# Eight image pairs through four layers on one core: layer 3 fed from padded copies, with the next pair's first scan step made inside it

## The chip, the cores and the metric

The kernel runs on one core of one Trainium2 chip. The metric is device time in microseconds (us). Five engines work beside each other, each through its own queue of instructions: TensorE (PE, matmul), VectorE (DVE), ScalarE (ACT), GpSimd (POOL) and SyncE (SP), which here only issues DMA transfers. SBUF is the on-chip memory of 128 partitions; PSUM holds what PE accumulates.

## What is computed

The input is 16 images of 192 channels and 64 x 64 points in float32. Four layers follow each other, each added to its own input, each with a group norm (32 groups of 6 channels) ahead of it:

```python
x = x + L0(gn(x))   # a small per-channel network: sigmoid differences
x = x + L1(gn(x))   # five shifted copies, 1x1 convolution 960 -> 192
x = x + L2(gn(x))   # selective scan, K = 4 directions, N = 16 states
x = x + L3(gn(x))   # depthwise convolutions, pointwise, batch norm, clip
```

The change is about the end of L2 and about L3:

```python
# L2: h = exp(delta * A) * h + delta * u * B ;  y = sum over n of C * h
# L3:
y = dw3x3(v) + dw5x5(v) + dw1x7(v) + dw7x1(v)
z = pointwise(y)                       # 192 -> 192
z = (z - mean(z)) / sqrt(var(z) + eps) # over all 16 images
return clip(gamma * z + beta, 0, 6)
```

## The kernel before, in words

**Tiling.** Two images of 192 channels make a pair of 384 rows: three tiles (NT = 3) of 128 partitions by 4096 points. There are eight pairs. After weights are prepared, `front(0)` does layers 0 and 1 and the projections of pair 0. Then `pair()` (L1161) runs for each pair `scans` (L783 to L1052) and `layer3` (L1053 to L1159). At the end the batch-norm sums of all pairs are combined and 24 tiles are streamed once more (L1230).

**Scans.** The loop has 768 steps: 3 tiles j, 4 directions, 4 chunks of 1024 points (48 values of t, the step's tile, direction and chunk) and 16 states n. A step is: `product` on DVE (pbt times du), `scan` on DVE, a copy of the last state on ACT, h times cb on POOL, a DMA that accumulates every fourth h onto its neighbour, and sums on PE into ysum, which ACT copies to X or Xt (Xt holds the transposed directions). Before each t, `step_rest` makes delta (PE matmul of dt, softplus on ACT) and du (POOL, delta times the normalised xn). All of this goes through wrappers (`_InOrder`, L51 and L64) that keep each engine's queue in program order, so that the profile gives one line, L64, to all of it. The front of the next pair is interleaved in the same loop, some instructions per step.

`finish(j)` closes a tile: four adds of Xt (transposed) to X, on POOL for tiles 0 and 1 and on DVE for tile 2, bn_stats of the sums on DVE, and the store of X to x3_d in DRAM. For tiles 0 and 1 it is spread over ten steps of the following tile; for tile 2 it stands behind the loop. The xn of the first tile is loaded and normalised, and the first delta and du are made, ahead of the loop; the first cb, bp and dt are loaded there too.

**Layer 3.** Here the instructions are not kept in program order: a scheduler places them on the queues. The parts are:

- xp (L1064): the three tiles are loaded from x3_d into the middle of 70 x 70 images, rows of 64 floats, whose edges POOL zeroes (L1070, L1072).
- diag (L1075): for each tile PE_TAPS = 7 diagonal matrices of 128 x 128, built on POOL from the identity, 21 instructions.
- `group_norm` (L337 to L369): bn_aggr on DVE, sums over groups on PE twice (gn_sum, 14 small matmuls each), small DVE operations between, and the power that gives rstd on POOL. `normalise` (L319) then works on DVE, in place, tile by tile.
- four chunks c of 1024 points, in each the three tiles j. The 29 taps are divided: 7 on PE as matmuls with the diagonals (L1111, two halves of 512 points), 8 on POOL (GP_TAPS; ACT scales a window, L1102, POOL adds it to g, L1106), and 14 on DVE (L1129), which adds to the PSUM tile l_p and writes the last sum to l_y. Four ident matmuls bring g into l_p (L1123).
- the pointwise matmuls zp (L1143) from the three l_y, a copy by ACT (L1150), bn_stats (L1151, zst) and the store of z to z_d (L1152).

One matmul instruction of float32 is two records in the trace. The PSUM tiles l_p have two buffers, the pointwise ones four banks. Memory is handed from one pool to the next, so that the first writer of a new tile waits for the last reader of what lay there.

Of the kernel before, what the change touches and what calls it, by code (L numbers as in the profile page):

```python
# [48 lines left out]
TAPS = [(3, 0), (3, 6), (0, 3), (6, 3)] + [(y, x) for y in range(1, 6) for x in range(1, 6)]  # L49
PE_TAPS = 7  # L50
GP_TAPS = 8  # L51
# [53 lines left out]
def conv_preact_kernel(ctx: ExitStack, tc: tile.TileContext, a: dict):  # L105
# [13 lines left out]
    wm_d = dram.tile([P, NG, P + GR], F32, name="wm_d")  # L119
    wt_d = dram.tile([GR, NG, 2 * P], F32, name="wt_d")  # L120

    const = ctx.enter_context(tc.tile_pool(name="const", bufs=1))
# [78 lines left out]
    with tc.tile_pool(name="prep", bufs=1) as prep, tc.tile_pool(  # L201
# [83 lines left out]
        for part, w in (  # L285
            (wc[:, :, 2:5, 2:5], w3x3),
            (wc[:, :, 3, :], w1x7),
            (wc[:, :, :, 3], w7x1),
        ):
            nc.vector.tensor_tensor(part, part, w, ALU.add)  # L290


# [16 lines left out]

    sets = [Made(n) for n in range(2)]  # L310

    def image(ap):
# [23 lines left out]

    def group_norm(E, st, stat, ps, gm, rstd):  # L337

        mv = stat.tile([P, NT, 2], F32, name="mv", tag="mv")
        mean = stat.tile([P, NT], F32, name="mean", tag="mean")  # L340
        d2 = stat.tile([P, NT], F32, name="d2", tag="d2")
        half = stat.tile([P, NT], F32, name="half", tag="half")
        E.dve.memset(half, -0.5)
        for j in range(NT):
            E.dve.bn_aggr(mv[:, j, :], st[:, j, :, :].rearrange("p c s -> p (c s)"))
        E.dve.tensor_copy(mean, mv[:, :, 0])

        def mean_of(src):
            s = ps("gn_sum")
            for jo in range(NT):  # L350
                for n, (b, ji) in enumerate(INTO[jo]):
                    E.pe.matmul(
                        s[:, jo : jo + 1],
                        grp[:, b, :],
                        src[:, ji : ji + 1],
                        start=(n == 0),
                        stop=(n == len(INTO[jo]) - 1),
                    )
                yield
            return s[:, :NT]  # L360

# [419 lines left out]

    def scans(i, o, st3, nxt):

        E = _Engines(tc, True)
        with ExitStack() as es:

            def pool(name, bufs, **kw):
                return es.enter_context(tc.tile_pool(name=name, bufs=bufs, **kw))

            one = pool("l2one", 1)  # L790
            two = pool("l2two", 2)
            hp = pool("l2h", 8)
# [6 lines left out]

            X = one.tile([P, L], F32, name="X")  # L800
            Xt = one.tile([P, L], F32, name="Xt")
# [16 lines left out]

            def load_bp(t):
                if t < T:  # L820
                    j, k, at, first = todo[t]
                    bps[t] = two.tile([BP, LC], BF16, name="bp")
                    E.sp.dma_start(out=bps[t], in_=o.bp[k, :, at : at + LC])

            def load_dt(t):
                if t < T:
                    j, k, at, first = todo[t]
                    dts[t] = one.tile([32 + RD, 512], F32, name="dt")
                    src, r = (o.dtp, RD * (k // 2)) if k % 2 else (o.dt, RD * (2 + k // 2))
                    for h in range(2):  # L830
                        E.sp.dma_start(
                            out=dts[t][32 * h : 32 * h + RD, :],
                            in_=src[r : r + RD, at + 512 * h : at + 512 * h + 512],
                        )

            def load_xn(j):
                if j < NT:
                    xns[j] = one.tile([P, L], F32, name="xn")
                    E.sp.dma_start(out=xns[j], in_=row_tiles(o.x2)[:, j, :])
# [27 lines left out]
            def step_rest(t):  # L867


                j, k, at, first = todo[t]  # L870
                dt = dts.pop(t)
                v = py.tile([P, LC], F32, name="v", tag="ysum")
                for h in range(2):
                    rows = slice(32 * h, 32 * h + RD)
                    E.pe.matmul(
                        v[:, 512 * h : 512 * h + 512],
                        dtw[rows, k, j, :],
                        dt[rows, :],
                        start=True,
                        stop=True,  # L880
                    )
                delta = two.tile([P, LC], F32, name="delta")
                E.table(SOFTPLUS)
                E.act.activation(delta, v, AF.Softplus, bias=dtb[:, k, j : j + 1])
                yield
                du = two.tile([P, LC], F32, name="du")
                E.gps.tensor_tensor(image(du), image(delta), seq(xns[j], k, at, LC), ALU.mult)
                made[t] = delta, du
# [74 lines left out]
            def finish(j):  # L963
# [12 lines left out]
                for at in range(10):  # L976
                    if at in (0, 2, 4, 6):
                        add(at // 2)
                    if at in (3, 5, 7, 9):
                        E.later(lambda c=at // 2 - 1: stats(c))  # L980
                    yield
                E.sp.dma_start(out=row_tiles(x3_d[i])[:, j, :], in_=X)

            load_xn(0)
            load_dt(0)
            load_bp(0)
            norm_xn(0)
            for _ in step_rest(0):
                pass
            load_dt(1)  # L990
            for s in range(3):
# [6 lines left out]
            fin = iter(())  # L998
            gstep = iter(())
            for s in range(total):  # L1000
                t, n = divmod(s, N)
# [3 lines left out]
                if n == 2:  # L1005
                    load_bp(t + 1)
                if n == 4:
                    load_dt(t + 2)
                if n == 6:
# [12 lines left out]
                if n > 4:  # L1022
                    next(fin, None)


# [22 lines left out]
            for g in (finish(NT - 1), fr):  # L1048
                for _ in g:
                    E.between()  # L1050
            E.between()

    def layer3(i, st3):  # L1053
        E = _Engines(tc, False)
        with tc.tile_pool(name="l3s", bufs=1) as stat, tc.tile_pool(name="l3x", bufs=1) as xk, tc.tile_pool(
            name="l3w", bufs=1
        ) as w_, tc.tile_pool(name="l3", bufs=2) as wk, tc.tile_pool(
            name="l3_pt", bufs=2, space=PSUM
        ) as pt, tc.tile_pool(name="l3_pz", bufs=4, space=PSUM) as pz:
            S = HW + 6  # L1060
            xp = xk.tile([P, NT, S, S], F32, name="xp")
            inside = slice(3, 3 + HW)
            for j in range(NT):
                nc.sync.dma_start(  # L1064
                    out=xp[:, j, inside, inside], in_=image(row_tiles(x3_d[i])[:, j, :])
                )
            pw = load("pw", [P, len(BLOCKS), P], w_)
            diag = w_.tile([P, NT, PE_TAPS, P], F32, name="diag")
            for edge in (slice(0, 3), slice(3 + HW, S)):
                nc.gpsimd.memset(xp[:, :, edge, :], 0.0)  # L1070
                for j in range(NT):
                    nc.gpsimd.memset(xp[:, j, inside, edge], 0.0)  # L1072
            for j in range(NT):
                for t, (ty, tx) in enumerate(TAPS[:PE_TAPS]):
                    nc.gpsimd.tensor_scalar(  # L1075
                        diag[:, j, t, :], ident, wc[:, j, ty, tx : tx + 1], None, ALU.mult
                    )
            gm = stat.tile([P, NT], F32, name="gm")
            rstd = stat.tile([P, NT], F32, name="rstd")
            banks = lambda name: pz.tile([P, 512], F32, name=name, tag="ps")  # L1080
            for _ in group_norm(E, st3, stat, banks, gm, rstd):
                pass
            for j in range(NT):
                v = xp[:, j, inside, inside]
                normalise(nc.vector, v, v, gm, rstd, j)
            zst = stat.tile([P, NT, 8, 6], F32, name="zst")
            def window(j, c, rows, tap):
                return xp[:, j, c + tap[0] : c + tap[0] + rows, tap[1] : tap[1] + HW]

            def factor(j, tap):  # L1090
                return wc[:, j, tap[0], tap[1] : tap[1] + 1]

            own = PE_TAPS + GP_TAPS
            for c in range(4):
                ys = []
                for j in range(NT):
# [59 lines left out]
            for j in range(NT):  # L1156
                nc.vector.bn_aggr(zmv[:, j, :], zst[:, j, :, :].rearrange("p c s -> p (c s)"))
            nc.sync.dma_start(out=zstat_d[i], in_=zmv.rearrange("p j s -> p (j s)"))

    def pair(i, q, more):  # L1160

        with tc.tile_pool(name="st3", bufs=1) as p3:
            st3 = p3.tile([P, NT, 8, 6], F32, name="st3")
            scans(i, sets[q], st3, None if more is None else (more, sets[1 - q]))
            layer3(i, st3)

    with tc.tile_pool(name="f_ps", bufs=1, space=PSUM) as ps:
        for _ in front(0, sets[0], _Engines(tc, False), Banks(ps, 8), True):
            pass
    for i in range(npair):  # L1170
        pair(i, i % 2, i + 1 if i + 1 < npair else None)

# [166 lines left out]
```

## Time and profile before

| | us |
|---|---|
| median of 3 runs | 28018.27 (28016.04 to 28032.98) |
| the profiled execution, its time | 28007.89 |
| its span, first to last instruction | 28006.0 |
| last scan of pair 0, end | 4172.6 |
| first scan of pair 1, start | 4538.5 |
| last scan of the last pair, end | 27270.8 |
| last zst of the last pair, end | 27617.3 |

The profiled execution is one run of the program under the hardware profiler; its rows are in microseconds from the first instruction. A row of the timeline gives start, length, engine, line, operation, what it writes and reads with shapes, how many instructions it joins, and in brackets the idle time ahead of it with what ended it. A row of windows gives a stretch and each engine's busy time in it, the clock that TensorE was granted as a share of the full one, and the share of DMA time. The mean granted clock of the run is 0.912.

In the scans a step takes 3.57 to 4.2 us. DMA is busy for 0.61 to 0.92 of the time there, more where the front of the next pair runs. Layer 3 takes four chunks of some 66 us with an opening ahead and a closing behind.

### The profile page before, as it was taken

What the parts mean: (1) busy time and instruction counts of PE and PEld (TensorE: products, weight loads), DVE (VectorE), ACT (ScalarE), POOL (GpSimd) and SP (SyncE); (2) the same over time, 40 slices, a digit from 0 to 9 for tenths busy, and PEclk for the clock granted to TensorE, in tenths of its full rate; (3) what the DMA queues carried; (4) which work ended last, traced back from release to release, by engine and by line L of the source; (5) the groups of instructions that cost most, each with busy time, mean ns of one, the idle gap of its engine ahead of it and who ended that gap; (6) DMA issues with size and microseconds to landing.
All of it is one profiled execution on the core that took longest, in us unless ns stands there. A gap on an engine that the chain in (4) does not pass through costs nothing. (4 is left out here: it accounts for less than half of the span.)

```text
span 28006.0 us, 208082 instructions
## 1 busy us (share of the span) xinstructions
PE 23305.0 (83%) x57140; PEld 9559.7 (34%) x57140; DVE 24196.3 (86%) x15397; ACT 16122.6 (58%) x23044; POOL 20813.2 (74%) x10440
## 2 busy tenths in 40 slices
PE   8799977999689986999779997899968998676663
PEld 4343323333233332333324332333323333222221
DVE  0399988999899998999989998899989999899994
ACT  7388445774468643785548844577446864344433
POOL 2388877887778876888768887788777887677772
PEclk9899988999899998999889998899989999888886
DMA  4489864898568973898748986589856897367765
GB/s 100 132 222 224 215 201 141 220 220 220 157 181 226 220 220 116 220 224 219 212 124 222 224 215 202 141 221 220 219 155 182 226 219 218 114 189 192 192 183 234
DMA packets 2008001, 5448.00 MB, mean 195 GB/s; under 512 B 550392, under 2 KB 550616, under 8 KB 1989424
## 3 DMA queue, kind: packets, MB, share of 16 engines
q1 hardware_dynamic: 1782192, 4578.95, 56.4%
q0 software_dynamic: 221184, 805.40, 15.2%
q10 hardware_dynamic: 3456, 50.33, 0.4%
q8 instruction: 455, 7.45, 0.1%
q14 instruction: 714, 5.85, 0.1%
HBM read 3896.19 MB, written 329.51 MB: 151 GB/s over the span
## 5 line engine op out<-in xcount | busy, mean ns | idle before, releaser
L64 POOL TENSOR_TENSOR h<-h,cb 128x1024 f32<-128x1024 f32 x6144 | 14856.3, 2464 | 4181.8 <-ACT state L64 3664.7
L64 DVE TENSOR_TENSOR_SCAN h<-dA,state,pbt 128x1024 f32<-128x1024 f32 x4608 | 10809.9, 2346 | 675.9 <-ACT dA L64 91.2
L64 PE MATMUL ysum<-h,ident 128*128 128x512 f32 x18432 | 9464.1, 639 | 208.2 <-DMA h<-h 138.6
L64 DVE TENSOR_TENSOR pbt<-du,pbt 128x1024 f32<-128x1024 f32 x6144 | 7434.8, 1210 | 658.0 <-PE pbt L64 619.6
L64 ACT ACTIVATE dA<-delta,t_alog 128x1024 f32<-128x1024 f32 x6144 | 7036.6, 1146 | 4.9
L64 PEld LDWEIGHTS ysum<-h,ident 128*128 128x128 f32 x18432 | 3777.4, 206 | 4520.3 <-issue 3923.8
L64 ACT COPY state<-h 128x1 f32<-128x1 f32 x6144 | 1145.0, 186 | 6401.7 <-DVE h L64 6324.1
L64 PE MATMUL pbt<-bp,pick 96*128 96x512 bf16 x8192 | 2686.3, 412 | 2127.4 <-DVE h L64 2106.9
L64 DVE TENSOR_TENSOR_SCAN h<-dA,pbt 128x1024 f32<-128x1024 f32 x1536 | 3509.1, 2285 | 228.5 <-DMA h<-h 52.6
L64 PE MATMUL p<-t,wts 96*128 96x512 f32 x5376 | 2707.6, 602 | 136.1 <-ACT t L64 135.9
L64 PE MATMUL p<-m,wms 128*96 128x512 f32 (+1 forms) x5376 | 2653.6, 595 | 0.9 <-ACT lu L64 0.3
L64 ACT ACTIVATE t<-p,bias 96x512 f32<-96x512 f32 x2688 | 1809.2, 679 | 1046.2 <-PE p L64 1027.8
L64 PEld LDWEIGHTS <-pick 96*128 96x128 bf16 x8192 | 711.9, 101 | 4920.9 <-DVE h L64 3256.2
L1106 POOL TENSOR_TENSOR l_g<-l_g,l_m 128x1024 f32<-128x1024 f32 x672 | 1615.1, 2405 | 452.3 <-ACT l_g L1102 346.6
L64 PE MATMUL l_p<-l_xp,w1s 128*128 128x512 f32 x3920 | 1844.7, 599 | 3.4 <-POOL l_xp L64 3.3
L1129 DVE SCALAR_TENSOR_TENSOR l_p<-xp,wc,l_p 128x1024 f32<-128x1024 f32 x1248 | 1589.8, 1287 | 262.6 <-PE l_p L1123 231.7
L64 PE MATMUL pbt<-bp,pick_mix 96*128 96x512 bf16 x4096 | 1282.7, 395 | 559.6 <-DVE h L64 555.3
L64 POOL DMA_DIRECT2D h<-h x1536 | 1359.0, 885 | 494.9 <-POOL h L64 427.9
L1111 PE MATMUL l_p<-xp,diag 128*128 128x512 f32 x2688 | 1289.0, 639 | 332.0 <-DVE l_y L1129 281.3
L64 PEld LDWEIGHTS p<-t,wts 96*128 96x128 f32 x5376 | 1007.9, 190 | 1292.6 <-issue 903.8
L64 ACT ACT_TABLE_LOAD x1111 | 1425.4, 1283 | 19.4
L64 POOL TENSOR_TENSOR du<-delta,xn 128x1024 f32<-128x1024 f32 x384 | 1034.5, 2694 | 452.7 <-ACT delta L64 452.7
(219 smaller groups left out, 17750.1 us busy)
## 6 DMA issues: line engine op xcount, KB each, us to landing
cb<-cp_d SPq DMA_DIRECT2D x2048, 512.0 KB
cb<-c_d SPq DMA_DIRECT2D x2048, 512.0 KB
h<-h POOLq DMA_DIRECT2D x1536, 512.0 KB, 7.1
cb<-cp_d SPq DMA_DIRECT2D x2048, 256.0 KB
cb<-c_d SPq DMA_DIRECT2D x2048, 256.0 KB
m<-l_xn SPq DMA_DIRECT2D x3072, 128.0 KB
bp<-bp_d SPq DMA_DIRECT2D x384, 192.0 KB
f0x<-in_x SPq DMA_DIRECT2D x96, 512.0 KB
```

The lines of the kernel that those rows point to most:

```text
L64: return self._tc.keep_in_program_order(call(*args, **kw))
L1106: nc.gpsimd.tensor_tensor(g, g, m, ALU.add)
L1111: nc.tensor.matmul(ps[:, cs], diag[:, j, t, :], window(j, 16 * c + 8 * h, 8, tap), start=(t == 0), stop=False,)
L1129: nc.vector.scalar_tensor_tensor(image(y if tap is TAPS[-1] else ps), window(j, 16 * c, 16, tap), factor(j, tap), image(ps), ALU.mult, ALU ...
```

## The change

- PE_TAPS is 8 instead of 7: DVE has 13 taps a tile and chunk.
- The diagonals are made once, in the preparation, stored to diag_d (1.57 MB) and loaded in each layer 3.
- xp_d in DRAM holds zero-padded 70 x 70 images of tiles 0 and 1. It is zeroed once. `finish` stores four strips of 16 rows (128 x 16 x 64) of each finished tile into it, beside the store to x3_d. Layer 3 loads tiles 0 and 1 whole from it.
- X lives on into layer 3: tile 2 is normalised from it straight into its padded image, and its store to x3_d is issued there.
- A second group norm over tiles 0 and 1 (gn0) is interleaved with the last 13 steps of the scans. No group of channels that tile 0 holds reaches tile 2, so tile 0 is normalised with it at once, in four strips of 16 rows.
- `begin(o_next)` loads the next pair's first xn, dt and bp and makes its delta and du; it is called ahead of chunk 2 of layer 3, and once behind `front(0)`. X, xn, bp, dt, delta and du lie in a pool `over` that lasts over all pairs.

```diff
-PE_TAPS = 7
+PE_TAPS = 8
...
+        zero = prep.tile([P, S, S], F32, name="zero")
+        nc.vector.memset(zero, 0.0)
+        for j in range(NT - 1):
+            nc.sync.dma_start(out=xp_d[j], in_=zero)
+        for j in range(NT):
+            diag = prep.tile([P, PE_TAPS, P], F32, name="diag", tag="diag", bufs=2)
+            for t, (ty, tx) in enumerate(TAPS[:PE_TAPS]):
+                nc.gpsimd.tensor_scalar(
+                    diag[:, t, :], ident, wc[:, j, ty, tx : tx + 1], None, ALU.mult
+                )
+            nc.sync.dma_start(out=diag_d[:, j, :, :], in_=diag)
...
+    def begin(o, psum):
+        E = _Engines(tc, False)
+        k = ORDER[0]
+        xn = over.tile([P, L], F32, name="xn")
+        nc.sync.dma_start(out=xn, in_=row_tiles(o.x2)[:, 0, :])
+        dt = load_dt(nc.sync, o, k, 0)
+        bp = load_bp(nc.sync, o, k, 0)
+        normalise(nc.vector, xn, xn, o.gm, o.rstd, 0)
+        delta = over.tile([P, LC], F32, name="delta", tag="delta", bufs=2)
+        make_delta(E, psum(), delta, dt, k, 0)
+        du = over.tile([P, LC], F32, name="du", tag="du", bufs=2)
+        nc.gpsimd.tensor_tensor(image(du), image(delta), columns(xn)[:, : LC // HW, :], ALU.mult)
+        return xn, bp, delta, du
...
                     if at in (3, 5, 7, 9):
-                        E.later(lambda c=at // 2 - 1: stats(c))
-                    yield
-                E.sp.dma_start(out=row_tiles(x3_d[i])[:, j, :], in_=X)
+                        c = at // 2 - 1
+                        E.later(lambda c=c: stats(c))
+                        if j < NT - 1:
+                            rows = slice(3 + 16 * c, 19 + 16 * c)
+                            E.sp.dma_start(
+                                out=xp_d[j][:, rows, 3 : 3 + HW],
+                                in_=image(X[:, 1024 * c : 1024 * c + 1024]),
+                            )
+                    yield
+                if j < NT - 1:
+                    E.sp.dma_start(out=row_tiles(x3_d[i])[:, j, :], in_=X)
...
+            gm0, rstd0 = (p3.tile([P, NT], F32, name=f"first{n}") for n in range(2))
+            gn0 = group_norm(E, st3, p3, ps, gm0, rstd0, range(2))
...
+                if t == T - 1 and n > 2:
+                    next(gn0, None)
...
-            xp = xk.tile([P, NT, S, S], F32, name="xp")
             inside = slice(3, 3 + HW)
-            for j in range(NT):
-                nc.sync.dma_start(
-                    out=xp[:, j, inside, inside], in_=image(row_tiles(x3_d[i])[:, j, :])
-                )
+            xps = {j: xk.tile([P, S, S], F32, name=f"xp{j}") for j in (2, 0, 1)}
+            for j in range(NT - 1):
+                nc.sync.dma_start(out=xps[j], in_=xp_d[j])
+            for r in range(0, HW, 16):
+                v = xps[0][:, 3 + r : 19 + r, inside]
+                normalise(nc.vector, v, v, gm0, rstd0, 0)
+            diag = w_.tile([P, NT, PE_TAPS, P], F32, name="diag")
+            nc.sync.dma_start(out=diag, in_=diag_d)
             pw = load("pw", [P, len(BLOCKS), P], w_)
-            diag = w_.tile([P, NT, PE_TAPS, P], F32, name="diag")
+            nc.sync.dma_start(out=row_tiles(x3_d[i])[:, NT - 1, :], in_=X)
...
-            for j in range(NT):
-                v = xp[:, j, inside, inside]
-                normalise(nc.vector, v, v, gm, rstd, j)
+            v = xps[1][:, inside, inside]
+            normalise(nc.vector, v, v, gm, rstd, 1)
+            normalise(nc.vector, xps[2][:, inside, inside], image(X), gm, rstd, 2)
...
+            begun = None
             for c in range(4):
+                if c == 2 and o_next is not None:
+                    begun = begin(o_next, lambda: pt.tile([P, 1024], F32, name="l3_p"))
```

## The prediction

> **What bounds the kernel now.** I read the busy table first, then the windows over the first pair's boundary (last scan of a pair to the first scan of the next), then its timeline, then DVE's waits.
>
> ```profile
> PE 23305.0 (83%) x57140; PEld 9559.7 (34%) x57140; DVE 24196.3 (86%) x15397; ACT 16122.6 (58%) x23044; POOL 20813.2 (74%) x10440
> ```
>
> DVE carries the kernel: its scans and products fill the 768 steps of a pair. The rest of a pair, layer 3, looks different. Columns: the stretch, its length, then busy time of each engine, granted clock, DMA share, GB/s.
>
> ```profile
> 4172.60:4218.80 46.20, 13.75 (x42) 8.76 (x41) 16.62 (x23) 1.20 (x2) 17.01 (x30) 0.61 0.44 120
> 4218.80:4320.60 101.80, 76.53 (x168) 30.60 (x170) 63.64 (x49) 52.45 (x49) 86.22 (x35) 0.86 0.17 42
> 4320.60:4386.90 66.30, 58.10 (x138) 23.24 (x136) 57.34 (x48) 31.20 (x30) 49.52 (x21) 0.92 0.06 24
> 4386.90:4452.60 65.70, 57.50 (x138) 23.06 (x136) 57.34 (x48) 31.07 (x30) 49.54 (x21) 0.92 0.06 24
> 4452.60:4519.30 66.70, 46.81 (x106) 18.45 (x102) 58.44 (x52) 10.09 (x13) 16.49 (x7) 0.85 0.06 26
> 4519.30:4538.50 19.20, 3.98 (x8) 1.04 (x8) 4.00 (x3) 5.90 (x6) 2.85 (x1) 0.53 0.62 218
> ```
>
> These sum to 365.9 us: an opening of 46.2 in which no engine is half busy, four chunks, and a closing of 19.2 in which the next pair's first step is loaded and made. The seven such gaps are 365.9 to 366.8, mean 366.2; the last pair, with no successor, needs 346.5 from its last scan to its last zst. The opening and the chunk that follows it, by their timeline (start, length):
>
> ```profile
> 4171.65 8.74 POOL L1075 TENSOR_SCALAR diag<-ident,wc 128x128 f32<-128x128 f32 x15
> ...
> 4180.37 2.33 POOL L64 TENSOR_TENSOR h<-h,cb 128x1024 f32<-128x1024 f32 x1
> ...
> 4197.15 0.32 SPq L64 DMA_DIRECT2D x_d<-X  x1
> 4203.46 20.00 SPq L1064 DMA_DIRECT2D xp<-x_d  x3
> ...
> 4218.78 14.73 PE L1111 MATMUL l_p<-xp,diag 128*128 128x512 f32 x28 [6.18 <-DVE xp L319]
> ...
> 4243.79 6.59 DVE L1129 SCALAR_TENSOR_TENSOR l_p<-xp,wc,l_p 128x1024 f32<-128x1024 f32 x5 [13.27 <-PE l_p L1123]
> ```
>
> The diagonals stand on POOL ahead of the last h multiply; behind that come the sums (to 4199.45), the store of X, the load of what was stored, its normalisation (4216.31, 2.41), and POOL's eight taps. DVE starts its taps 71.2 after the last scan (4172.6). Times below with a plus count from that scan.
>
> **The opening.** In the built order of the changed kernel POOL runs the last h multiply at once: it ends at +2.6 instead of +10.1. PE's sum (3.54), ACT's copy (1.01) and DVE's adds and statistics (12.07) follow as now, to +19.3. Tile 0 loads from xp_d as soon as the multiply has released its memory; the nearest row, 2 MB of contiguous xn, takes 9.1 from issue to normalisation, so it is there at about +12. Its four strips take 2.5 (2.41 as one), to +21.8. The full group norm takes 8.9 to the end of its second PE sums as now: +30.7. Tile 0's conv stands behind them on PE: 32 records of 128x512 instead of 28 at 0.44, 2.3 of cold clock, 1.93 for the ident matmuls, so DVE's first tap is at +49.3. POOL has g(j0) by +44.4 (two adds before the rstd power, five behind it, 2.4 each), inside that. Tile 1 and 2 are normalised (3.45 and 3.93) in DVE's wait. Gain so far 21.9.
>
> **The first chunk** is now paced by POOL, 86.2 busy of 101.8, since each tile's g costs 19.3 there. POOL starts 25 earlier and ends g(j2) at +83; I get the end of chunk 0 at +114.3 against +149.3, 35.0 earlier.
>
> **The eighth tap.** A steady chunk of before, first DVE's, then PE's part:
>
> ```profile
> 4409.77 13.21 DVE L1129 SCALAR_TENSOR_TENSOR l_p<-xp,wc,l_p 128x1024 f32<-128x1024 f32 x10
> 4423.01 1.28 DVE L1129 SCALAR_TENSOR_TENSOR l_y<-xp,wc,l_p 128x1024 f32<-128x1024 f32 x1
> 4426.59 2.61 DVE L1129 SCALAR_TENSOR_TENSOR l_p<-xp,wc,l_p 128x1024 f32<-128x1024 f32 x2 [2.30 <-PE l_p L1123]
> ```
> ```profile
> 4410.00 14.68 PE L1111 MATMUL l_p<-xp,diag 128*128 128x512 f32 x28 [7.65 <-DVE l_y L1129]
> 4424.61 1.93 PE L1123 MATMUL l_p<-l_g,ident 64*64 64x512 f32 x8
> ```
>
> DVE loses three instructions of 1.29 a chunk, 3.9. But the ring it sits in closes through PE: tile 2's conv waits for a PSUM buffer that l_y of tile 0 frees, and takes 14.68 for 28 records, 2.3 of it a cold start after 7.65 idle (the mean over 24 such gaps; after gaps under 1.5 nothing is lost). With 32 records it adds 1.75. In the new order the next conv is also cut by the pointwise matmuls: 12 of its 16 instructions stand ahead of them, 4 behind, 3.5 on the path from l_y of tile 2 to the next tap. PE's idle gap shrinks to some 4, so I give the cold start 0.8. Ring: 35.4 from the chunk's first tap to tile 2's, 20.35 for that tile, 9.2 to the next: 65.0, against 65.7 to 66.7. Nearly all of the tap is given back; without the cut it would be 61.5.
>
> [...]
>
> **The closing.** xn, dt, bp are fetched in the scans, and delta and du are made between chunks 1 and 2. The first scan of the next pair now waits only for the last z store to land: 7.2 from the last l_y to its issue, 3.4 to its landing, where before 27.1 lay between that l_y and the scan. In exchange chunk 1 to 2 waits: delta stands on ACT behind three scaled windows, one waiting for POOL, and its PSUM buffer is the one that tile 0's conv needs, whose last nine instructions stand behind four pointwise ones. I get 14.4 more for that chunk. So chunk starts are +114.3, +193.7 (65.0 + 14.4), +258.7; tile 2's taps +294.1, l_y +312.3, first scan +323. Against 366.2: **-43.2** a pair, -302 for seven. The last pair has no such step: 114.3 + 130 + 35.4 + 18.25 + 8.25 = 306.2 against 346.5, -40.
>
> **What moves into the scans.** DVE does the xn normalisation (3.3, between the 2.41 and 3.47 of its rows) and the small operations of the early group norm (2.3) where its pitch leaves no room: 3.56 to 3.60 in the last steps for 1.21 + 2.35. That is +5.6 for seven pairs and 2.3 for the last: +41. The loads fall where DMA is at 0.61 and cost nothing; if they did, their 9.1 would come back. Diagonals and zeroing in the opening weights delay POOL by some 6 to 9, which the early start of pair 0's first step (xn load to scan 16.5, about 7.5 saved) pays back: +2, between -8 and +10.
>
> **The strips.** Four stores per tile into xp_d, 128x16x64 of 256-byte rows, eight a pair, on SP's queue ahead of the cb loads, each waiting for its X add on POOL (for whose lateness the next cb load, two steps ahead, has some 7). The trace of before has no store of such rows. Its loads of 256-byte packets (layer 1's windows, 239616 of them) take 24 ns a packet: 2048 / 16 x 25 ns = 3.2 a strip. Ends: nothing if hidden, 25.6 a pair if all is exposed. The stretch of tile 0's strips has little room, that of tile 1's has:
>
> ```profile
> 8870.00:9860.00 990.00, 919.78 (x2344) 387.32 (x2343) 926.70 (x565) 655.15 (x966) 835.53 (x424) 0.97 0.92 220
> 9860.00:10690.00 830.00, 677.00 (x1631) 270.43 (x1630) 758.47 (x469) 399.19 (x572) 630.62 (x309) 0.90 0.73 213
> ```
>
> I take two thirds of tile 0's four: 8.5 a pair, 1 in the last: +60.
>
> [...]
>
> **Sum.** -302 - 40 + 41 + 2 + 60 = -239 on the profiled 28007.9 (span 28006.0): 27769. The median shown is 10.4 above the profiled time, so **27780**.
>
> **Rivals.** (1) Strips hidden and the cold start gone: -60 and some -26 (0.8 a chunk): 27690. (2) PE is worse than I built it: the cold clock costs its full 2.3 in each ring (+1.5 x 32 = 48) and begin 8 more a pair (+56): 27885. DVE's 13.3 wait behind PE speaks for it, the shorter gap against. (3) The other side: strip stores at over 4.7 each. Without them the change is worth 299, 37.4 a pair; eight at 4.7 eat it, at 5.5 the kernel is slower by over 0.2%; at 6.4, twice the load's packets, it is 27719 (the sum without strips, at the median) + 8 x 8 x 6.4 = 28130. The 0.92 of DMA speaks for it, the 0.73 of tile 1's stretch and the 24 ns against. (4) Padded copies that come no earlier, because the load of tile 0 waits for memory held to the end of the sums: tile 0 is then ready at +19.3 + 9.1 + 2.5 = +31, PE no later than forecast but POOL's chain 8 later, 64 in all: 27845.
>
> **How the numbers follow.** The forecast with what lies between it and (4): 0.62; (1) 0.13; (2) or strips at the full 25.6 (+120, 27900): 0.12; between these and no change counted with no change, 0.06; (3) 0.07. Range 27680 to 27910. 0.2% is 56 us, about what a measurement of this kernel can tell from no change: faster 0.87, same 0.06, slower 0.07.
>
> **What would show it.** In the profile after: first l_p at +49 (wrong above +56), chunk cycle 65, the chunk with delta 79, gaps of 323; in the scans the steps behind 272 longer by 8, those behind 528 not. A chunk of 61.5 would refute the cut conv, unchanged steps behind 272 the price of the strips, and a gap above 340 the closing.

## The result, and the profile after

The changed kernel takes 28164.89 us (median of 5, 28149.86 to 28170.34) against 28018.27 for the kernel before: a ratio of 1.0051, 95% interval 1.0036 to 1.0065. It is slower, by 147 us; forecast were 238 us less. The profiled execution has a span of 28148.1, 142.1 more than before.

The share of busy time tells nothing of it:

```profile
PE 23517.4 (84%) x57652; PEld 9661.5 (34%) x57652; DVE 24161.9 (86%) x15398; ACT 16120.1 (57%) x23044; POOL 20709.2 (74%) x10272
```

DVE does less work than before (24161.9 against 24196.3) in a longer span. I cut both traces at the same instructions, the first and last scan of each pair. The gaps between pairs are 352.1 to 353.6 now (365.9 to 366.8 before), so layer 3 did become shorter, by 13.3 a pair and, in the last pair, by 12.8 to its last zst and 14.4 to the end of the program: 108 in all, a third of the 342 forecast. The scans became longer, by 247 in eight pairs. These are the windows over the same boundary as before:

```profile
4210.00:4241.80 31.80, 11.78 (x42) 8.30 (x41) 18.12 (x25) 7.82 (x8) 7.99 (x7) 0.66 0.76 288
4241.80:4341.00 99.20, 79.44 (x177) 32.17 (x178) 62.94 (x48) 45.83 (x43) 82.40 (x34) 0.87 0.03 11
4341.00:4419.60 78.60, 61.75 (x144) 24.52 (x143) 54.05 (x46) 33.33 (x32) 52.37 (x22) 0.87 0.05 20
4419.60:4493.40 73.80, 67.17 (x160) 27.39 (x159) 54.10 (x46) 30.94 (x30) 49.56 (x21) 0.95 0.05 22
4493.40:4558.50 65.10, 52.41 (x125) 20.65 (x124) 54.24 (x48) 10.06 (x12) 16.50 (x7) 0.90 0.12 44
4558.50:4563.50 5.00, 0.00 (x0) 0.00 (x0) 1.50 (x2) 1.72 (x3) 0.00 (x0) 0.83 0.58 183
```

The opening fell from 46.2 to 31.8 and the closing from 19.2 to 5.0, as meant. But the first chunk still takes 99.2 (101.8), and the two in the middle, whose windows are cut at the last zst of each, grew to 78.6 and 73.8. DVE is busy for only 54 in each: it waits. For what, its waits over this boundary say (released by, us in total, times, longest):

```profile
DVE zst L1205 <- ACT z L1204: 52.1, 20, 16.4
DVE l_p L1183 <- PE l_p L1177: 33.3, 9, 9.1
DVE X L64 <- ACT X L64: 7.2, 1, 7.2
```

The same view of before, for a boundary of the same pair:

```profile
DVE l_p L1129 <- PE l_p L1123: 28.8, 9, 13.3
DVE zst L1151 <- ACT z L1150: 22.5, 20, 3.0
DVE X L64 <- ACT X L64: 14.8, 1, 14.8
```

The wait for X was halved by the move of the diagonals. The wait of bn_stats (zst) for ACT's copies of z rose from 22.5 to 52.1, and one instance from 3.0 to 16.4. It stands in the first chunk. DVE there, by the timeline:

```profile
4261.00 14.54 DVE L1183 SCALAR_TENSOR_TENSOR l_p<-xp,wc,l_p 128x1024 f32<-128x1024 f32 x11 [9.11 <-PE l_p L1177]
...
4298.26 2.61 DVE L1183 SCALAR_TENSOR_TENSOR l_p<-xp,wc,l_p 128x1024 f32<-128x1024 f32 x2 [2.08 <-PE l_p L1177]
4317.23 0.70 DVE L1205 BATCH_NORM_STATS2 zst<-z 128x6 f32<-128x512 f32 x1 [16.36 <-ACT z L1204]
```

and ACT in the same time:

```profile
4314.51 1.17 ACT L1156 ACTIVATE l_m<-xp,wc 128x1024 f32<-128x1024 f32 x1 [1.28 <-POOL l_g L1160]
4315.58 1.15 ACT L1156 ACTIVATE l_g<-xp,wc 128x1024 f32<-128x1024 f32 x1
4316.64 0.56 ACT L1204 COPY z<-zp 128x512 f32<-128x512 f32 x1
```

The first tap is at 4261.00, +51.1 (last scan 4209.9), 20 earlier than before. DVE reaches its first bn_stats at +91 and stands there until +107. The copy it needs takes 0.56, and its matmuls were over at +90; but on ACT's queue it stands behind all eight scaled windows of the next chunk's first tile (l_m, l_g), and these wait for buffers, of which POOL frees one every 2.4. The same two copies hold PE, whose pointwise matmuls for z's third tile need the banks that they read:

```profile
4317.25 2.08 PE L1197 MATMUL zp<-l_y,t_pw 128*128 128x512 f32 x2 [11.98 <-ACT z L1204]
4323.32 2.08 PE L1197 MATMUL zp<-l_y,t_pw 128*128 128x512 f32 x2 [4.00 <-ACT z L1204]
4325.19 11.10 PE L1165 MATMUL l_p<-xp,diag 128*128 128x512 f32 x24
```

The next conv stands behind them; its first 24 records end at +126.3, DVE's last l_y of the chunk at +125.8. So DVE and PE come out of their waits together, and which of the two sets the chunk is not separated.

In the scans the loss is in three places. Counted from the first scan of a pair and averaged over pairs 0 to 6, the changed kernel is 1.5 ahead at step 272, 13.4 behind at step 280, 7.7 at step 518, 20.8 at step 534, 22.1 at step 745 and 31.8 at the last. The first two jumps are where `finish` stores its strips (16 DRAM stores of before for the eight pairs' tiles 0 and 1 became 80), the third, behind step 745, is the xn normalisation (3.4) and the early group norm (6.3).

### The profile page after: what moved, and what is told of

The parts are those of the page before. It is cut to its first block, busy times and chain, and to the rows that moved or that the text cites. A ratio compares the mean times of both kernels' runs of the same rounds, so it can differ in the third digit from the quotient of the medians.

```text
span 28148.1 us, 208907 instructions
## 1 busy us (share of the span) xinstructions
PE 23517.4 (84%) x57652; PEld 9661.5 (34%) x57652; DVE 24161.9 (86%) x15398; ACT 16120.1 (57%) x23044; POOL 20709.2 (74%) x10272
## 5 line engine op out<-in xcount | busy, mean ns | idle before, releaser
L1183 DVE SCALAR_TENSOR_TENSOR l_p<-xp,wc,l_p 128x1024 f32<-128x1024 f32 x1152 | 1484.1, 1288 | 294.6 <-PE l_p L1177 259.3
L1165 PE MATMUL l_p<-xp,diag 128*128 128x512 f32 x3072 | 1447.9, 629 | 164.5 <-DVE l_y L1183 85.4
L1156 ACT ACTIVATE l_m<-xp,wc 128x1024 f32<-128x1024 f32 x672 | 778.2, 1160 | 960.9 <-POOL l_g L1160 960.9
```

Of the source, the lines that this page charges most:

```text
L1156: nc.scalar.activation(image(m), window(j, 16 * c, 16, tap), AF.Copy, scale=factor(j, tap))
L1165: nc.tensor.matmul(ps[:, cs], diag[:, j, t, :], window(j, 16 * c + 8 * h, 8, tap), start=(t == 0), stop=False,)
L1183: nc.vector.scalar_tensor_tensor(image(y if tap is TAPS[-1] else ps), window(j, 16 * c, 16, tap), factor(j, tap), image(ps), ALU.mult, ALU ...
```

## The experiments

The kernel before was measured again beside each group of runs: 28014.49 beside the first four, 28031.82 beside the next four, 28020.24 beside the last four. The ratios are to these; a difference between runs of two groups can be off by as much as these are, up to 17.

**Without the strips.**

```diff
-                            E.sp.dma_start(
-                                out=xp_d[j][:, rows, 3 : 3 + HW],
-                                in_=image(X[:, 1024 * c : 1024 * c + 1024]),
-                            )
...
-                nc.sync.dma_start(out=xps[j], in_=xp_d[j])
+                nc.sync.dma_start(
+                    out=xps[j][:, inside, inside], in_=image(row_tiles(x3_d[i])[:, j, :])
+                )
```

> The changed kernel without the strip stores: no padded copies in DRAM, tiles 0 and 1 of layer 3 are loaded from x3_d into padded images whose edges POOL zeroes; all else as changed. Theory (the stores of 256-byte rows take DMA time that the scans' loads need): the 23.5 us a pair that the scans lost between their step 272 and step 735 go, 15.7 in the last pair, so about 180 in all and 27985 us; tile 0 lands by about +16, still ahead of the sums that end at +19, so layer 3 keeps its time. Rival (the loss in the scans comes from the other moved work, loads of the next pair and early group norm): under 40 us are won, 28125 or more.

Measured: 27961.6 us, ratio to before 0.9982 (0.9972 to 0.9991). That is 203 less than the changed kernel. Of the 179 between the two profiled spans 166 lie in the scans and 12 ahead of the first, where this run leaves out the zeroing of xp_d; layer 3 keeps its time (gaps within 0.5 but for one).

**The same strips with long rows.**

```diff
-                                out=xp_d[j][:, rows, 3 : 3 + HW],
-                                in_=image(X[:, 1024 * c : 1024 * c + 1024]),
+                                out=xq_d[j][:, 1024 * c : 1024 * c + 1024],
+                                in_=X[:, 1024 * c : 1024 * c + 1024],
```

> The changed kernel with its strip stores kept in number, bytes, place on SP's queue and waits, but into an unpadded copy, so that each store has 128 rows of 4 KB instead of 2048 of 256 bytes; layer 3 loads tiles 0 and 1 from it into padded images. Theory (the short rows are the price): within 30 us of the kernel without strips, about 28000. Rival (SP waits in each strip for an X add on POOL, and the loads behind it come late): as the changed kernel, 28150 to 28165. A second rival (the bytes themselves): half the loss stays, 28075.

Measured: 27969.2 us, 0.9985 (0.9976 to 0.9995), 8 us from the kernel without strips. So neither the bytes, nor SP's waits for the X adds, nor their place in the queue cost anything to speak of: the 256-byte rows of the padded copy do. Whether it is their length alone, or also that they start 280 bytes apart in DRAM, was not separated: this run changed both. The DMA packets of the changed kernel and of this one:

```profile
DMA packets 2131604, 5490.60 MB, mean 195 GB/s; under 512 B 682568, under 2 KB 682792, under 8 KB 2109696
```
```profile
DMA packets 2014579, 5478.98 MB, mean 196 GB/s; under 512 B 551464, under 2 KB 551688, under 8 KB 1994976
```

The 131104 more packets under 512 B are the 64 strips of 2048 rows. Summing the trace's packets of 256 bytes, before has 239616 at 23.7 ns, all loads; the changed kernel 131072 more, which take 48.5 ns each: 6.2 us of all 16 engines for a strip that I had priced at 3.2. The mean comes from a tail: in the 36 strips with no load of layer 1's windows near them half of the packets take 29 ns or less (22 for the loads of before), but 24% take over 40, on average 116, against 1.6% of the loads. The steps of tile 1's strips in pair 1, before and after:

```profile
6533.70:6611.40 77.70, 66.93 (x163) 28.27 (x162) 65.45 (x49) 24.35 (x36) 68.45 (x34) 0.93 0.76 221
```
```profile
6571.40:6660.40 89.00, 70.04 (x163) 29.20 (x161) 65.50 (x49) 24.57 (x36) 68.96 (x34) 0.88 1.07 221
```

Before, 0.24 of 77.7 us was free, 18.6: room for four strips at 3.2 (12.8), not at 6.2 (24.8). (The share sums packet times; at the 1.07 of the second row packets of one engine must have overlapped.) In tile 0's steps of the same pair the share was 0.84 of 69.2 us, 11 free; they grew to 84.6.

What waits for it in the steps 266 to 282 of pair 1 is not what one would look for first:

```profile
ACT m L64 <- DMA m<-l_xn: 19.6, 3, 10.8
...
PE ysum L64 <- ACT delta L64: 11.3, 1, 11.3
...
DVE h L64 <- ACT dA L64: 7.3, 1, 7.3
```

A load of the next pair's front comes late, ACT stands in it, and dA and delta behind it on ACT's queue hold DVE and PE. In the same steps of before none of these three waits is listed.

**Seven taps in the changed kernel.**

```diff
-PE_TAPS = 8
+PE_TAPS = 7
```

> The changed kernel with seven taps on TensorE as before, 14 on DVE. Theory (a steady chunk is not bounded by DVE's taps but by a ring: ident of tile 0, POOL's sums, the second z copy on ACT that stands behind scaled windows waiting for POOL, its bn_stats 46.5 after the chunk's first tap, the taps behind it and PE's way to the next chunk): the taps behind it grow by 1.3, the way over PE shrinks by 3.4, since the conv again stands whole ahead of the pointwise matmuls, so 2.1 less a chunk, 45 to 50 in all: 28115. Rival (the prediction's ring over DVE and PE): 0.7 more a chunk, 28180. Rival (DVE's instruction count decides): 3.9 more a chunk, 28280.

Measured: 28138.7 us, 1.0045 (1.0029 to 1.0062), 26 us less than the changed kernel, by medians whose intervals overlap. The traces say it more plainly: the seven gaps are 26 shorter in all and the last pair's end 1, though the scans of this profiled execution happen to be 25 longer. The sign and the steady chunk are the theory's: in the last pair chunk 1 to 2 takes 66.3 against 68.4. The size is half, because the last chunk, behind which no conv waits, grew: 58.6 from its first tap to its last l_y in the first seven pairs, against 54.4. The eighth tap costs here; it does not give the 0.7 of the prediction.

**Statistics read from PSUM.**

```diff
-                        nc.vector.bn_stats(zst[:, jo, 2 * c + h, :], z[:, 512 * h : 512 * h + 512])
+                        nc.vector.bn_stats(zst[:, jo, 2 * c + h, :], ps)
```

> The changed kernel with bn_stats of z read from the PSUM tile that the pointwise matmuls wrote, not from the copy that ACT makes. Theory (DVE is held by z copies that stand on ACT's queue behind windows waiting for POOL, 16.4 us in the first chunk): first chunk some 15 shorter, the steady ones 63 instead of 68.4, 25 a pair, 200 in all: 27965. Rival (POOL's own sums, 86 busy of 102 in the first chunk, bound it whoever reads z): within 20 us of the changed kernel, 28150.

Measured: 28189.1 us, 1.0065 (1.0050 to 1.0080). The edit did not take the wait away. DVE:

```profile
4319.49 0.70 DVE L1205 BATCH_NORM_STATS2 zst<-zp 128x6 f32<-128x512 f32 x1 [16.35 <-ACT z L1204]
```

and ACT's copy of that bank, which ends at 4319.46:

```profile
4318.90 0.56 ACT L1204 COPY z<-zp 128x512 f32<-128x512 f32 x1
```

The second reader of the bank began when the first had ended, so the test told nothing of the theory. PE also waited: the pointwise matmuls of z's third tile need a bank that the late copies free, and the next conv, behind them in PE's queue, began only at +115.6 (last pair; +114.8 in the changed kernel). A fair test had to take the copies off ACT, for both engines.

**DVE copies z** (in the kernel without strips, as all that follow but the last but one).

```diff
-                        nc.scalar.copy(z[:, 512 * h : 512 * h + 512], ps)
+                        nc.vector.tensor_copy(z[:, 512 * h : 512 * h + 512], ps)
```

> The kernel without strip stores (tiles 0 and 1 loaded from x3_d), with the copies of z from PSUM made by DVE instead of ACT, so that neither bn_stats nor the pointwise banks wait for ACT's queue. The run before this one that read the statistics from PSUM did not do what it said: bn_stats still began only when ACT's copy of the same bank had ended, and PE still waited for a bank. Theory (ACT's in-order queue, whose z copies stand behind windows that wait for POOL, holds DVE and PE): the first chunk 20 to 23 shorter, each following one some 5 although DVE has six copies more, 35 a pair, 280 in all: 27680. Rival (POOL's sums bound the chunks themselves, three times 19.3 and 5 more): at most 8 a pair, 27900 or more. Rival (DVE's added 3.6 a chunk is on the path and nothing is released): 28070.

Measured: 27840.5 us, 0.9934 (0.9919 to 0.9949): 121 (by the medians) less than without the edit, less than the theory's 280 and far more than either rival's. The trace divides it. The first taps of chunk 1 come at +115.0 instead of +134.9, and a steady chunk of the last pair takes 64.2 instead of 68.3, both as expected and both with more work on DVE. But the chunk with begin takes 92.9 instead of 83.0: in pair 0 PE has delta's sum ready at +161 instead of +186, and nine windows then still stand ahead of delta on ACT instead of four; it comes at +184.6, and the conv waits for its PSUM tile. Whether it was DVE's wait or PE's that counted in the first chunk stays open, since the edit frees both.

**begin behind the chunks.**

```diff
-                if c == 2 and o_next is not None:
-                    begun = begin(o_next, lambda: pt.tile([P, 1024], F32, name="l3_p"))
...
+            if o_next is not None:
+                begun = begin(o_next, lambda: pt.tile([P, 1024], F32, name="l3_p"))
             zmv = stat.tile([P, NT, 2], F32, name="zmv")
```

> The kernel without strip stores, with begin called behind the four chunks instead of ahead of chunk 2: the next pair's xn, dt and bp are still fetched in the scans, but delta's PSUM tile is taken when no conv of a later chunk needs one. Theory (the 14.7 by which chunk 1 to 2 is longer come from that PSUM buffer and the delta on ACT behind POOL-paced windows): that chunk falls from 83.0 to 68.3, the tail grows by 0 to 3 for the table loads, 12 to 15 a pair in seven pairs, 27865. Rival (the cost only moves to the end, as the 16 that lay behind the last z before): 27960.

Measured: 27888.0 us, 0.9952 (0.9937 to 0.9966), 74 less; the chunk fell from 83.0 to 68.0 and the seven gaps by 108 in all (the last pair took 4 longer to the end of the program, and the scans are 19 longer in this trace). It is the theory's, a little smaller by the medians.

**Without the early group norm.**

```diff
-                if t == T - 1 and n > 2:
-                    next(gn0, None)
...
-                normalise(nc.vector, v, v, gm0, rstd0, 0)
+                normalise(nc.vector, v, v, gm, rstd, 0)
```

> The kernel without strip stores and without the early group norm in the scans: tile 0 is normalised in its four strips behind the full group norm. Theory (the early norm costs in the scans about what it gives in layer 3): the scans lose 6.5 to 7 a pair less; the first tap comes 6 later (first normalisation at +32 instead of +19, POOL's eight taps of tile 0 in 19 instead of 26.7, since no power stands in them); net within 1 a pair, 27955 to 27970. Rival (tile 0 at once is worth its 13 of normalisation time): 7 a pair worse, 28015. Rival (the first chunk is bounded by other things than tile 0): 7 a pair better, 27905.

Measured: 27959.9 us, 0.9975 (0.9966 to 0.9985), 2 from the kernel with it. The first tap moved from +50.7 to +56.0, the last third of the scans lost 54 less in all.

**DVE's copies and begin behind the chunks together.**

> Without strip stores, with DVE's copies of z and with begin behind the chunks, the two edits together. If the two waits are separate, their gains add: 280 and 100 on 27962, 27580. If both free the same queue (ACT), the second gives less: about 27640. If POOL bounds the chunks, 27850 or more.

Measured: 27636.7 us, 0.9860 (0.9844 to 0.9877): 325 less than without the two, more than 121 + 74, because the two waits met in one chunk: chunk 1 to 2, at 92.9 with DVE's copies alone, takes 62.6. It beats both kernels. Its first chunk on DVE:

```profile
4258.43 2.61 DVE L1173 SCALAR_TENSOR_TENSOR l_p<-xp,wc,l_p 128x1024 f32<-128x1024 f32 x2 [2.09 <-PE l_p L1167]
...
4266.31 0.69 DVE L1195 BATCH_NORM_STATS2 zst<-z 128x6 f32<-128x512 f32 x1
```

From the two taps to the second bn_stats are 8 us with no idle time between; in the changed kernel they were 25 (4298.26 to 4323.31).

**Seven taps in that kernel.**

```diff
-PE_TAPS = 8
+PE_TAPS = 7
```

> The kernel of the run before (no strip stores, z copied by DVE, begin behind the chunks) with seven taps on TensorE instead of eight. Theory (the eighth tap was worth nothing only because ACT's queue set the chunk; with that queue out of the way the ring over DVE and PE counts): the first l_y comes 3.4 later, tile 2's taps 4 later and last 1.3 longer, the way to the next chunk is 1 shorter: 4 more a chunk, 110 in all, 27750. Rival (PE's order gives the tap back here too, as the seven-tap run on the changed kernel showed): 27640 or less.

Measured: 27780.7 us, 0.9915 (0.9901 to 0.9930): 144 slower than with eight (142 of it in the gaps and the last pair's end). One and the same edit wins some 27 us in layer 3 where ACT's queue sets the chunk and loses 142 there where it does not.

**The full group norm in that kernel**, the edit of the run above on the group norm.

> The kernel without strip stores, with z copied by DVE and begin behind the chunks, and without the early group norm (tile 0 behind the full one). Theory: the scans win 6.5 to 7 a pair, 54; the first tap is 5 later, 42; 27625. Rival (in the faster layer 3 tile 0 at once is worth its whole 13): 27690.

Measured: 27618.5 us, 0.9856 (0.9841 to 0.9871): at the theory's 27625, within the interval of the kernel with the early norm. It pays what it costs here too.

**DVE copies z in the kernel before**, the one-line edit alone.

> The kernel before with one edit: DVE makes the six copies of z in a chunk. Theory (with seven taps the ring over DVE and PE and the one over ACT's queue were about as long, so freeing ACT releases little, and DVE takes 3.6 a chunk more): between 28000 and 28060. Rival (ACT's queue alone held layer 3 before the change too): 120 faster, 27900.

Measured: 28059.0 us, 1.0013 (1.0003 to 1.0023). Before the change ACT's queue was not alone in holding layer 3: DVE's longest wait for it was 3.0. Freeing it made chunk 0 to 1 shorter (73.4 against 78.1), and DVE's six copies made each following chunk longer (68.2 against 66). The change moved the bound to ACT: it made tile 0 early, and so DVE reaches its bn_stats before the windows ahead of the copies are through.

**begin outside layer 3.**

```diff
-                if c == 2 and o_next is not None:
-                    begun = begin(o_next, lambda: pt.tile([P, 1024], F32, name="l3_p"))
...
+            with tc.tile_pool(name="b_ps", bufs=1, space=PSUM) as bs:
+                begun = begin(sets[q], lambda: bs.tile([P, LC], F32, name="b_v"))
             first = scans(i, sets[q], p3, st3, X, begun, nxt)
```

> The kernel without strip stores and with z copied by DVE, in which the next pair's first step is made behind layer 3, ahead of the next loop, as in the kernel before. Theory (begin is worth the 16 that lie behind the last l_y more than with it, less the 3.3 of xn's normalisation in the scans): 12 to 13 a pair slower than the kernel with begin behind the chunks, 27725. Rival (begin is worth nothing wherever it stands): 27640.

Measured: 27650.4 us, 0.9868 (0.9854 to 0.9883), 14 from the kernel with begin behind the chunks. The theory's number failed, but the edit was not what I took it for: xn is still normalised between steps 745 and 750 (3.4 there, as before the edit), so its load was still hoisted into the scans, and only delta and du moved. What begin as a whole is worth was not tried by leaving it out.

## Why the prediction was wrong, step by step

| term, us over the run | forecast | measured |
|---|---|---|
| layer 3, gaps between the scans | -342 | -108 |
| strips | +60 | +181 |
| xn's normalisation and the early group norm, in the scans | +41 | +74 |
| preparation | +2 | +3 |
| elsewhere in the scans | 0 | -9 |

The measured terms come from the two traces: the strips from what is lost between steps 272 and 745 (23.6 a pair, 16 in the last), the others as told above; the first row counts the last pair to the end of the program; with 1 of rounding they make the 142.

**The first chunk** is the step that failed most. The first tap was right (+49.3 forecast, +51 measured), and so was POOL's end of g(j2) (+83, +85). "I get the end of chunk 0 at +114.3" was wrong by 20.7 (+135.0 in the last pair), 165 over eight pairs: I followed the data of tile 2 and left out that two z copies stand on ACT behind the next chunk's windows. POOL ends chunk 1's first tile 16 earlier than before (+104 against +120), and a DVE that came 20 earlier, and a PE with it, had to wait for it through ACT. Taking the copies off ACT brought +115.0.

**The steady ring**, "nearly all of the tap is given back", 65.0, measured 68.4. The cut of the conv was seen rightly: 9.2 forecast from the last l_y to the next tap, 9.1 to 9.6 measured in the last pair (5.7 in a steady chunk of before). So was what I called the cold start of tile 2's conv, 0.8 for a gap of some 4: the gap shrank to 2.67, and its 32 records take 15.17 behind it on average, against 14.61 after gaps under 1.5. But the ring that closed last ran over the ident of tile 0, POOL, the second z copy and its bn_stats, 46 to 47 after the chunk's first tap in both kernels; only nine tap instructions stand behind it now instead of ten. So the tap saved 1.3 and, by the cut conv, cost 3.5 to 3.8. The steady chunk with seven taps, 66.3, confirmed it; with the copies off ACT the chunk is 64.2, and there the tap was worth 144.

**The closing** was right: 14.4 forecast for begin between the chunks, 14.0 measured (82.4 on average from chunk 1 to 2, against 68.4 in the last pair, which has none), 10.7 forecast from the last l_y to the first scan, 11.4 measured. Together with 3.4 for xn that is no gain: 16 saved behind the chunks for 17 spent. The sign set for it, "a gap above 340", was met by the gaps of 353, but the chunks made them.

**The strips**: "3.2 a strip" was the price of a loaded row for a stored one; stored it is 6.2. "That of tile 1 has [room]" was a right reading (0.73 over the stretch, 0.76 in the steps themselves), but the room was for strips at 3.2: tile 1's strips cost 13, tile 0's 15, of which 6 came back later. Rival 3 named the cause and, at 6.4 each all exposed, overpriced it: 2.8 of each was exposed. That its 28130 lies near the measured 28165 is luck, since it overpriced the gain of layer 3 as well; without the strips the kernel is still only 0.18% faster than before. (Its "at 5.5 the kernel is slower by over 0.2%" is 53 us, 0.19%.) The slowdown needed both failures. That a stored packet takes twice a loaded one, as in the 6.4 of rival 3, no run had shown; measured in its place is a mean of 48.5 ns against 23.7 for a load of the same size, 6.2 a strip. But half of the packets are near a load's time (in the 36 strips above 29 ns or less, against 22), the mean is made by a quarter of them (24% over 40, on average 116), and no run shows what holds these.

**What moved into the scans**: xn at 3.3 was right (3.4). The early norm at 2.3 was 6.3, told below.

## What to carry to other kernels

When a stage is made to start earlier, walk every in-order queue that its later instructions pass, also on engines far from busy, and ask behind whose waits each of them stands: here ACT, busy for 57%, held DVE, busy for 86%. A change in the number of instructions on the busiest engine is worth what the ring that closes last makes of it, and that can be read only from the interval between two of its waits; the same tap lost some 27 us or won 144. Price a DRAM store from a row of a store with rows of the same length (here 48.5 ns a packet, against 23.7 for the loads), and hold the DMA time that it adds against the DMA time that is free in the steps in which it falls: here 24.8 us against 18.6.

## What the runs showed of the hardware

Two DVE instructions on two numbers a partition took until POOL's multiply beside them had ended. In the scans of the changed kernel, DVE:

```profile
4160.69 2.12 DVE L64 COPY mean<-mv 128x2 f32<-128x2 f32 x1
```

and POOL:

```profile
4160.44 2.34 POOL L64 TENSOR_TENSOR h<-h,cb 128x1024 f32<-128x1024 f32 x1 [1.22 <-ACT state L64]
```

Both end at 4162.8; d at 4170.44 took 2.20 in the same way, beside a multiply that ended at 4172.6. In the run without the early group norm the full one finds POOL idle, and the same operations, there on three numbers, take 0.17 and 0.16:

```profile
4181.43 0.17 DVE L362 COPY mean<-mv 128x3 f32<-128x3 f32 x1
4185.49 0.16 DVE L383 TENSOR_TENSOR d<-d,mv 128x3 f32<-128x3 f32 x1
```

The two differences, 1.95 and 2.04, make the 4.0 between the 6.3 that the early norm cost and the 2.3 forecast. Not every small instruction was held: a BATCH_NORM_AGGREGATE at 4160.34, which began 0.10 before the same multiply and ended beside it, took 0.32. Why these two lasted until POOL's multiply had ended, no run here tells. A bn_stats of a PSUM bank that ACT was to copy began when the copy had ended (4319.49 after 4319.46); whether the chip or the order set at build time asks for that, the runs do not tell.
